# Squares of two chunks on row halves, V0 and V1 terms on quarters of the array, in a compressed-interaction kernel

## Chip, cores, metric

The kernel runs on one core of a Trainium2 chip. The metric is the device time of one execution in microseconds (us), the median of several runs. The profile adds TensorE's weight loads (PEld) to the engines PE (TensorE), DVE (VectorE), ACT (ScalarE), POOL (GpSimd) and SP (the queue of loads).

## The reference, cut to what matters

```python
def _cin_forward(x, Ws, bs, fc_w, fc_b, split_half=True):
    x0 = x; h = x; xs = []
    for i in range(3):                                   # cut
        z = jnp.einsum('bfe,bge->bfge', x0, h).reshape(Bn, f0 * fh, e)
        y = jnp.einsum('oc,bce->boe', Ws[i], z) + bs[i][None, :, None]
        if i != 2: x_i, h = y[:, :64, :], y[:, 64:, :]
        else:      x_i, h = y, y
        xs.append(x_i)
    return jnp.sum(jnp.concatenate(xs, axis=1), axis=2) @ fc_w.T + fc_b
```

x is 1024 x 64 x 16 in fp32, the hidden sizes are 64, the result is 1024 x 1. Everything after h1 is linear in the weights that follow, so the kernels fold W1, W2 and fc_w into one form M, and W0, W1 and fc_w into two 64 x 64 forms V0 and V1. What remains per element is h1 (64 rows), q = M(x, x) + V1 x (64 rows), and y = V0 x (64 rows): sum over (h1 + b) q + (y + c) x.

## The kernel before

The 32 batch rows of a chunk are laid out as 512 columns, there are 32 chunks. The 64 x 64 products x_f x_g are symmetric, so they are computed as 16 shifted products on 128 rows (`z`) and one square (the lower 64 rows of `zl`); each is multiplied by a 128 x 128 weight whose first 64 columns give h1 and whose last 64 give q.

```python
    def products(c, j):
        z = zp.tile([128, NI, N], F32, tag="z", name="z")
        nc.vector.tensor_tensor(z, xas[c], xbs[c][:, j, :]..., ALU.mult)
        for i in range(NI):
            t = j * NI + i
            nc.tensor.matmul(accs[c], w_all[:, t, :], z[:, i, :], start=(t == 0), stop=False)

    def squares(c):        # rows 0-63: x squared; rows 64-127: x itself, weights V1
        nc.scalar.activation(zls[c][0:64], xas[c][0:64, 0, :], AF.Square)
        nc.tensor.matmul(accs[c], w_all[:, NT, :], zls[c], start=False, stop=True)

    def combine(c):        # cut
        nc.scalar.copy(q, accs[c][64:128])
        nc.vector.scalar_tensor_tensor(uu[to, 0, :], accs[c][0:64], bh1, q, ALU.add, ALU.mult)
        if half == 0:
            return
        y = ps.tile([128, N], F32, tag="y", name=f"y_{c}", bufs=1)
        nc.tensor.matmul(y, bd, xxs[c // 2], start=True, stop=True)     # bd = diag(V0, V0)
        nc.vector.scalar_tensor_tensor(uu[:, 1, :], y, cx, xxs[c // 2], ALU.add, ALU.mult)
        nc.vector.tensor_reduce(acc[:, :, c // 2, :], uu..., AX.X, ALU.add)

    for c in range(NCH + 1):
        load_chunk(c + 1)                                   # cut: bounds
        products(c, 0); products(c, 1)
        combine(c - 1)
        products(c, 2); products(c, 3); squares(c)
```

The set-up makes the weights on the chip: `pv2` and `pm` matmuls (V2 form and M), M out to memory (`md`) and back in skewed form (`ms1`, `ms2`), summed into `w_all`; and V0 and V1 as one row:

```python
    for k in range(4):
        w01 = setup.tile([128, 1024], F32, tag="w01", name=f"w01_{k}")     # 2 buffers
        nc.sync.dma_start(out=w01, in_=wv01[:, k * 1024 : (k + 1) * 1024])
        for m in range(2):
            pv = ps.tile([2, 512], F32, tag="set", name=f"pv_{k}_{m}", bufs=4)
            nc.tensor.matmul(pv, fc01, w01[:, m * 512 : (m + 1) * 512], start=True, stop=True)
            nc.scalar.copy(vrow[:, col : col + 512], pv)
    # then transfers of vrow's two rows into w_all[64:128, NT, 64:128] (V1) and bd (V0, twice)
```

In the traces an engine's instructions don't always stand in the order of the source.

Of the kernel before, what the change touches and what calls it, by code (L numbers as in the profile page):

```python
# [23 lines left out]
F32 = mybir.dt.float32  # L27
AF = mybir.ActivationFunctionType
ALU = mybir.AluOpType
AX = mybir.AxisListType  # L30

F = 64
E = 16
B = 1024
CB = 32
N = CB * E
# [3 lines left out]
NT = NI * NJ  # L40
# [4 lines left out]
def cin_kernel(ctx, tc, x2, w0a, w0b, w1h, wv2, wv01, b0, b1, b2, fc_w, fc_b, out):  # L45
    nc = tc.nc
    const = ctx.enter_context(tc.tile_pool(name="const", bufs=1))
    setup = ctx.enter_context(tc.tile_pool(name="setup", bufs=2))
    xp = ctx.enter_context(tc.tile_pool(name="xp", bufs=3))
    zp = ctx.enter_context(tc.tile_pool(name="zp", bufs=3))  # L50
    sp = ctx.enter_context(tc.tile_pool(name="sp", bufs=2))
    ps = ctx.enter_context(tc.tile_pool(name="ps", bufs=2, space=bass.MemoryType.PSUM))
    dr = ctx.enter_context(tc.tile_pool(name="dr", bufs=1, space=bass.MemoryType.DRAM))

    def rows(c, first, dims):

        return bass.AP(
            tensor=x2.tensor,
            offset=(c * 2 * F + first) * N,
            ap=[[N, F]] + [[n * N, k] for n, k in dims] + [[1, N]],  # L60
        )
# [5 lines left out]
    nc.scalar.dma_start(out=fc2, in_=fc_w[0, 128:256].unsqueeze(1))  # L67
    nc.scalar.dma_start(out=fc01[0:64, 0:1], in_=fc_w[0, 0:64].unsqueeze(1))
    nc.scalar.dma_start(out=fc01[64:128, 1:2], in_=fc_w[0, 64:128].unsqueeze(1))
    bh1 = const.tile([F, 1], F32, tag="bh1", name="bh1")  # L70
    bh2 = const.tile([F, 1], F32, tag="bh2", name="bh2")
    bcol = const.tile([128, 2], F32, tag="bcol", name="bcol")
    fcol = const.tile([128, 2], F32, tag="fcol", name="fcol")
    fcb = const.tile([1, 1], F32, tag="fcb", name="fcb")
    b0c = b0.unsqueeze(1)
    b1c = b1.unsqueeze(1)
    nc.gpsimd.dma_start(out=bh1, in_=b0c[64:128])
    nc.gpsimd.dma_start(out=bh2, in_=b1c[64:128])
    nc.gpsimd.dma_start(out=bcol[0:64, 0:1], in_=b0c[0:64])
    nc.gpsimd.dma_start(out=bcol[64:128, 0:1], in_=b1c[0:64])  # L80
# [1 line left out]
    for j in range(2):  # L82
        nc.gpsimd.dma_start(
            out=fcol[:, j : j + 1], in_=fc_w[0, j * 128 : (j + 1) * 128].unsqueeze(1)
# [6 lines left out]
    nc.gpsimd.memset(ones[64:128, 1:2], 1.0)  # L91


    w_all = const.tile([128, NT + 1, 128], F32, tag="w_all", name="w_all")
    bd = const.tile([128, 128], F32, tag="bd", name="bd")
    nc.gpsimd.memset(w_all[64:128, NT, 0:64], 0.0)
    nc.gpsimd.memset(bd, 0.0)


    w2s = const.tile([128, 32, 128], F32, tag="w2s", name="w2s")  # L100
# [4 lines left out]
        nc.sync.dma_start(out=w2s[:, 8 * k : 8 * k + 8, :], in_=wv2[:, 8 * k : 8 * k + 8, :])  # L105
    nc.sync.dma_start(out=w1s, in_=w1h)

    xas, xbs, zls, xxs = {}, {}, {}, {}

    def load_chunk(c):  # L110
        xa = xp.tile([128, NI, N], F32, tag="xa", name=f"xa_{c}")
        xb = xp.tile([128, NJ, N], F32, tag="xb", name=f"xb_{c}")
        zl = xp.tile([128, N], F32, tag="zl", name=f"zl_{c}")
        for half in range(2):
            to = slice(half * F, (half + 1) * F)
            nc.sync.dma_start(out=xa[to], in_=rows(c, 0, [[1, NI]]))
            nc.sync.dma_start(out=xb[to], in_=rows(c, 16 * half + 4, [[4, NJ]]))
        nc.sync.dma_start(out=zl[F:128], in_=rows(c, 0, []))
        if c % 2 == 0:
            xxs[c // 2] = sp.tile([128, N], F32, tag="xx", name=f"xx_{c}")  # L120
        to = slice(c % 2 * F, (c % 2 + 1) * F)
        nc.sync.dma_start(out=xxs[c // 2][to], in_=rows(c, 0, []))
        xas[c], xbs[c], zls[c] = xa, xb, zl

    load_chunk(0)
    nc.sync.dma_start(out=w0t, in_=w0a)
# [1 line left out]


    v2t = const.tile([128, F], F32, tag="v2t", name="v2t")  # L130
    pv2 = ps.tile([128, 32], F32, tag="set", name="pv2", bufs=4)
    for k in range(32):
        nc.tensor.matmul(pv2[:, k : k + 1], w2s[:, k, :], fc2, start=True, stop=True)  # L133
    for half in range(2):
# [7 lines left out]
    for m in range(4):  # L142
        for half in range(2):
            to = slice(half * F, (half + 1) * F)
            pm = ps.tile([F, 512], F32, tag="set", name=f"pm_{m}_{half}", bufs=4)
            nc.tensor.matmul(  # L146
                pm, v2t[to], w1s[to, m * 512 : (m + 1) * 512], start=True, stop=True
            )
            f0 = half * 32 + m * 8
            m_to = m_sb[:, f0 : f0 + 8, :].rearrange("p f g -> p (f g)")  # L150
            if half:
                nc.vector.tensor_copy(m_to, pm)  # L152
            else:
                nc.scalar.copy(m_to, pm)
# [10 lines left out]
    def skewed(first, dims):  # L165
        return bass.AP(
            tensor=md.tensor, offset=md.offset + first, ap=[[row + F, F]] + dims
        )

    for half in range(2):  # L170
        to = slice(half * F, (half + 1) * F)
        b = 16 * half + 4
# [4 lines left out]
        for i in range(NI):  # L177
# [1 line left out]
                out=ms2[to].rearrange("p (j i) g -> p j i g", i=NI)[:, :, i, :],  # L179
                in_=skewed(i * row + b * F, [[4 * F, NJ], [1, F]]),  # L180
            )
    nc.scalar.dma_start(out=w_all[0:64, NT, 64:128], in_=skewed(0, [[1, F]]))

    nc.vector.memset(ms2[64:128, 3 * NI, :], 0.0)  # L184
    nc.vector.memset(w0u[64:128, 3 * NI, :], 0.0)
    nc.vector.tensor_tensor(w_all[:, 0:NT, 0:64], w0t[:, 0:NT, :], w0u, ALU.add)
    nc.vector.tensor_copy(w_all[0:64, NT, 0:64], w0t[0:64, NT, :])
    nc.vector.tensor_tensor(w_all[:, 0:NT, 64:128], ms1, ms2, ALU.add)  # L188


    vrow = const.tile([2, F * F], F32, tag="vrow", name="vrow")
    for k in range(4):
        w01 = setup.tile([128, 1024], F32, tag="w01", name=f"w01_{k}")
        nc.sync.dma_start(out=w01, in_=wv01[:, k * 1024 : (k + 1) * 1024])
        for m in range(2):
            pv = ps.tile([2, 512], F32, tag="set", name=f"pv_{k}_{m}", bufs=4)
            nc.tensor.matmul(pv, fc01, w01[:, m * 512 : (m + 1) * 512], start=True, stop=True)  # L197
            col = (2 * k + m) * 512
            nc.scalar.copy(vrow[:, col : col + 512], pv)  # L199
    nc.scalar.dma_start(  # L200
        out=w_all[64:128, NT, 64:128], in_=vrow[1:2, :].rearrange("o (f g) -> o f g", g=F)
    )
    for half in range(2):
        to = slice(half * F, (half + 1) * F)
        nc.scalar.dma_start(
            out=bd[to, to], in_=vrow[0:1, :].rearrange("o (f g) -> o f g", g=F)
        )


    cx = const.tile([128, 1], F32, tag="cx", name="cx")  # L210
    pcx = ps.tile([128, 1], F32, tag="set", name="pcx", bufs=4)
    for half in range(2):
        nc.tensor.matmul(
            pcx[half * F : (half + 1) * F], v2t[0:64], bh2, start=True, stop=True
        )
    nc.scalar.copy(cx, pcx)
    cst = const.tile([1, 1], F32, tag="cst", name="cst")
    pc = ps.tile([1, 1], F32, tag="set", name="pc", bufs=4)
    for j in range(2):
        nc.tensor.matmul(  # L220
            pc, fcol[:, j : j + 1], bcol[:, j : j + 1], start=(j == 0), stop=(j == 1)
# [2 lines left out]


    acc = const.tile([128, 2, NCH // 2, CB], F32, tag="acc", name="acc")
    accs, uus = {}, {}

    def products(c, j):
        z = zp.tile([128, NI, N], F32, tag="z", name="z")  # L230
        nc.vector.tensor_tensor(  # L231
            z, xas[c], xbs[c][:, j, :].unsqueeze(1).to_broadcast([128, NI, N]), ALU.mult
        )
        for i in range(NI):
            t = j * NI + i
            nc.tensor.matmul(accs[c], w_all[:, t, :], z[:, i, :], start=(t == 0), stop=False)  # L236

    def squares(c):
        nc.scalar.activation(zls[c][0:64], xas[c][0:64, 0, :], AF.Square)  # L239
        nc.tensor.matmul(accs[c], w_all[:, NT, :], zls[c], start=False, stop=True)  # L240

    def combine(c):
        half = c % 2
        to = slice(half * F, (half + 1) * F)
        if half == 0:
            uus[c // 2] = sp.tile([128, 2, N], F32, tag="uu", name=f"uu_{c}")
        uu = uus[c // 2]
        q = sp.tile([F, N], F32, tag="q", name=f"q_{c}")
        nc.scalar.copy(q, accs[c][64:128])  # L249
        nc.vector.scalar_tensor_tensor(uu[to, 0, :], accs[c][0:64], bh1, q, ALU.add, ALU.mult)  # L250
        if half == 0:
            return
        y = ps.tile([128, N], F32, tag="y", name=f"y_{c}", bufs=1)
        nc.tensor.matmul(y, bd, xxs[c // 2], start=True, stop=True)  # L254
        nc.vector.scalar_tensor_tensor(uu[:, 1, :], y, cx, xxs[c // 2], ALU.add, ALU.mult)  # L255
        nc.vector.tensor_reduce(  # L256
            acc[:, :, c // 2, :], uu.rearrange("p k (b e) -> p k b e", e=E), AX.X, ALU.add
        )

    for c in range(NCH + 1):  # L260
        if c + 1 < NCH:
            load_chunk(c + 1)
        if c < NCH:
            accs[c] = ps.tile([128, N], F32, tag="acc", name=f"acc_{c}")
            products(c, 0)
            products(c, 1)
        if c > 0:
            combine(c - 1)
        if c < NCH:
            products(c, 2)  # L270
            products(c, 3)
            squares(c)

    res = const.tile([1, B], F32, tag="res", name="res")
    half_pairs = NCH // 4
    for k in range(2):
        po = ps.tile([1, 2, half_pairs * CB], F32, tag="set", name=f"po_{k}", bufs=4)
        pairs = slice(k * half_pairs, (k + 1) * half_pairs)
        for half in range(2):
            for n in range(2):  # L280
                nc.tensor.matmul(  # L281
                    po[:, half, :],
                    ones[:, half : half + 1],
                    acc[:, n, pairs, :],
                    start=(half == 0 and n == 0),
                    stop=(half == 1 and n == 1),
                    skip_group_check=True,
                )
        nc.scalar.activation(  # L289
            res[:, k * 512 : (k + 1) * 512].rearrange("o (m h b) -> o h m b", h=2, b=CB),  # L290
            po.rearrange("o h (m b) -> o h m b", b=CB),
            AF.Identity,
            bias=cst,
        )
# [46 lines left out]
```

## Time and profile before

| | before |
|---|---|
| median of the runs | 554.62 us (552.36 to 554.69) |
| TensorE busy | 515.9 us of a span of 555.0 |
| VectorE, ScalarE busy | 352.0 and 44.9 us |
| first product matmul starts | 66.25 us |
| one pair of chunks in the loop | 30.04 us |

The lines that carry it are shown in the prediction. Read the table as two parts: a start of 66 us in which the weights are made, with TensorE waiting for more than half of it (31.3 us busy), and a loop in which TensorE never waits.

### The profile page before, as it was taken

To read this page: it belongs to the slowest core of one execution; us is meant where nothing else is said; L and a number is where in the kernel's file an instruction comes from. 1 tells how busy PE (TensorE), PEld (TensorE's weight loads), DVE (VectorE), ACT (ScalarE), POOL (GpSimd) and SP (SyncE) were. 2 spreads that over 40 slices of the span, in tenths; PEclk is the share of its full clock that TensorE was granted. 3 is DMA by queue.
4 is the path that set the end of the run, shared out by engine and by line. 5 is a ranking of instruction groups with operands and counts; after the bars stand their busy time and mean duration, and the time that the engine had idled before them with its cause. 6 is when DMAs were issued, how large, how long until landed. Compare 5 with 4: busy or idle time off the path is not lost.

```text
span 555.0 us, 3402 instructions
## 1 busy us (share of the span) xinstructions
PE 515.9 (93%) x1240; PEld 231.9 (42%) x1240; DVE 352.0 (63%) x205; ACT 44.9 (8%) x81; POOL 5.3 (1%) x18
## 2 busy tenths in 40 slices
PE   5803799999999999999999999999999999999997
PEld 5600144444444444444444444444444444444442
DVE  0250076768677677768676867767776867686751
ACT  0100300000000000000000000000000000000001
POOL 3000000000000000000000000000000000000000
PEclk9967699999999999999999999999999999999999
DMA  8999998787777777877778777777787877874000
GB/s 254 185 283 210 205 208 170 144 163 146 156 153 159 150 152 162 180 161 161 160 147 165 146 154 154 154 150 154 161 180 161 165 155 151 162 152 77 0 1 0
DMA packets 33114, 85.33 MB, mean 154 GB/s; under 512 B 6405, under 2 KB 6949, under 8 KB 28710
## 3 DMA queue, kind: packets, MB, share of 16 engines
q1 hardware_dynamic: 29234, 81.84, 71.1%
q10 hardware_dynamic: 3608, 3.28, 2.8%
q8 instruction: 10, 0.16, 0.2%
q14 instruction: 6, 0.05, 0.0%
q0 software_dynamic: 256, 0.00, 0.0%
HBM read 82.89 MB, written 2.17 MB: 153 GB/s over the span
## 4 chain that ended last, share of the span: by engine, by line
PE 92%; DMA 6%; DVE 0%; ACT 0%; issue 0%; ACTq 0%; SPq 0%
PE acc L236 79%; PE acc L240 5%; DMA w<-in_wv 3%; PE pv L133 2%; PE y L254 2%; PE pv L197 2%; DMA ms<-md 1%; DMA fc<-in_fc_w 1%; DMA md<-m_sb 1%; PE pm L146 1%; PE po L281 0%; DVE acc L256 0%; DVE uu L255 0%; ACT res L289 0%; ACT q L249 0%
## 5 line engine op out<-in xcount | busy, mean ns | idle before, releaser
L236 PE MATMUL acc<-z,w_all 128*128 128x512 f32 x1024 | 447.2, 592 | 0.0
L231 DVE TENSOR_TENSOR z<-xa,xb 128x2048 f32<-128x2048 f32 x128 | 293.3, 2292 | 135.9 <-PE acc L236 134.6
L236 PEld LDWEIGHTS acc<-z,w_all 128*128 128x128 f32 x1024 | 194.5, 190 | 244.5 <-issue 244.4
L249 ACT COPY q<-acc 64x512 f32<-64x512 f32 x32 | 18.6, 582 | 443.8 <-PE acc L240 443.8
L197 PE MATMUL pv<-w,fc 128*2 128x512 f32 x16 | 11.5, 887 | 27.9 <-DMA w<-in_wv 14.9
L240 PE MATMUL acc<-zl,w_all 128*128 128x512 f32 x64 | 32.7, 592 | 0.0
L250 DVE SCALAR_TENSOR_TENSOR uu<-acc,bh,q 64x512 f32<-64x512 f32 x32 | 23.7, 740 | 10.0 <-ACT q L249 9.5
L239 ACT ACTIVATE zl<-xa 64x512 f32<-64x512 f32 x32 | 20.1, 628 | 3.6 <-DMA xa<-in_x 3.6
L133 PE MATMUL pv<-fc,w2s 128*128 128x1 f32 x64 | 13.8, 352 | 6.6 <-DMA fc<-in_fc_w 6.6
L256 DVE TENSOR_REDUCE acc<-uu 128x64 f32<-128x1024 f32 x16 | 19.5, 1220 | 0.5
L240 PEld LDWEIGHTS acc<-zl,w_all 128*128 128x128 f32 x64 | 12.2, 190 | 15.3 <-issue 15.3
L197 PEld LDWEIGHTS pv<-w,fc 128*2 128x2 f32 x16 | 1.6, 108 | 37.6 <-issue 21.5
L133 PEld LDWEIGHTS pv<-fc,w2s 128*128 128x128 f32 x64 | 13.7, 332 | 6.6 <-DMA fc<-in_fc_w 6.6
L254 PE MATMUL y<-xx,bd 128*128 128x512 f32 x32 | 16.3, 592 | 0.0
L136 DVE COPY v2t<-pv 64x32 f32<-64x32 f32 x2 | 0.4, 184 | 20.4 <-PE pv L133 20.4
L255 DVE SCALAR_TENSOR_TENSOR uu<-y,cx,xx 128x512 f32<-128x512 f32 x16 | 11.9, 745 | 0.0
L188 DVE TENSOR_TENSOR w_all<-ms,ms 128x1024 f32<-128x1024 f32 x1 | 1.2, 1224 | 13.2 <-DMA ms<-md 13.2
L254 PEld LDWEIGHTS y<-xx,bd 128*128 128x128 f32 x32 | 6.1, 190 | 7.7 <-issue 7.7
L199 ACT COPY vrow<-pv 2x512 f32<-2x512 f32 x8 | 4.2, 570 | 33.3 <-DMA ms<-md 32.2
L184 DVE MEMSET ms<- 64x64 f32 x1 | 0.1, 112 | 9.7 <-DMA ms<-md 9.7
L146 PE MATMUL pm<-w1s,v2t 64*64 64x512 f32 x16 | 5.6, 809 | 0.5 <-DVE v2t L137 0.5
L152 DVE COPY m_sb<-pm 64x512 f32<-64x512 f32 x4 | 2.7, 683 | 3.2 <-PE pm L146 3.2
(33 smaller groups left out, 21.0 us busy)
## 6 DMA issues: line engine op xcount, KB each, us to landing
xa<-in_x SPq DMA_DIRECT2D x64, 512.0 KB, 5.8
xb<-in_x SPq DMA_DIRECT2D x64, 512.0 KB, 7.1
zl<-in_x SPq DMA_DIRECT2D x32, 128.0 KB, 4.2
xx<-in_x SPq DMA_DIRECT2D x32, 128.0 KB, 4.1
w2s<-in_wv SPq DMA_DIRECT2D x4, 512.0 KB, 7.8
w<-in_wv SPq DMA_DIRECT2D x4, 512.0 KB, 11.9
w1s<-in_w1h SPq DMA_DIRECT2D x1, 1024.0 KB, 13.4
md<-m_sb ACTq DMA_DIRECT2D x2, 512.0 KB, 7.1
```

Source lines behind the costliest of these rows:

```text
L133: nc.tensor.matmul(pv2[:, k : k + 1], w2s[:, k, :], fc2, start=True, stop=True)
L146: nc.tensor.matmul(pm, v2t[to], w1s[to, m * 512 : (m + 1) * 512], start=True, stop=True)
L197: nc.tensor.matmul(pv, fc01, w01[:, m * 512 : (m + 1) * 512], start=True, stop=True)
L231: nc.vector.tensor_tensor(z, xas[c], xbs[c][:, j, :].unsqueeze(1).to_broadcast([128, NI, N]), ALU.mult)
L236: nc.tensor.matmul(accs[c], w_all[:, t, :], z[:, i, :], start=(t == 0), stop=False)
L239: nc.scalar.activation(zls[c][0:64], xas[c][0:64, 0, :], AF.Square)
L240: nc.tensor.matmul(accs[c], w_all[:, NT, :], zls[c], start=False, stop=True)
L249: nc.scalar.copy(q, accs[c][64:128])
L250: nc.vector.scalar_tensor_tensor(uu[to, 0, :], accs[c][0:64], bh1, q, ALU.add, ALU.mult)
L254: nc.tensor.matmul(y, bd, xxs[c // 2], start=True, stop=True)
L255: nc.vector.scalar_tensor_tensor(uu[:, 1, :], y, cx, xxs[c // 2], ALU.add, ALU.mult)
L256: nc.vector.tensor_reduce(acc[:, :, c // 2, :], uu.rearrange("p k (b e) -> p k b e", e=E), AX.X, ALU.add)
```

## The change

The intent: TensorE spends 35 full matmuls a pair of chunks, 32 on products, 2 on squares (whose lower 64 rows carry V1) and 1 on y. Squares alone need 64 rows, V0 and V1 need 64 rows and 64 columns each. So the change squares both chunks of a pair at once and runs the two squares matmuls on the two row halves of the array side by side, and the four V terms (V0 and V1 of two chunks) on its four quarters: 34 units instead of 35. For the four V terms to fall on four different quarters the odd chunk must have its h1 and q halves swapped, which needs a third block of weight columns.

```diff
-    w_all = const.tile([128, NT + 1, 128], F32, tag="w_all", name="w_all")
-    bd = const.tile([128, 128], F32, tag="bd", name="bd")
+    w_all = const.tile([128, NT, 192], F32, tag="w_all", name="w_all")   # h1 | q | h1
+    w_sq = const.tile([128, 128], F32, tag="w_sq", name="w_sq")
+    w_x = const.tile([128, 128], F32, tag="w_x", name="w_x")
 ...
+    nc.scalar.copy(w_all[:, :, 128:192], w_all[:, :, 0:64])
 ...     # set-up PSUM tiles: bufs=4 becomes bufs=3; accumulators: 2 become 4
-            pv = ps.tile([2, 512], F32, tag="set", name=f"pv_{k}_{m}", bufs=4)
+            pv = ps.tile([2, 512], F32, tag="set", name=f"pv_{k}_{m}", bufs=3)
 ...
+    def begin(k):
+        xx = xxs[k]
+        sq = sp.tile([128, N], F32, tag="sq", name=f"sq_{k}")
+        nc.scalar.activation(sq, xx, AF.Square)
+        ys[k] = ps.tile([128, N], F32, tag="y", name=f"y_{k}", bufs=1)
+        for half in range(2):
+            to = slice(half * F, (half + 1) * F)
+            acc_c = ps.tile([128, N], F32, tag="acc", name=f"acc_{2 * k + half}", bufs=4)
+            accs[2 * k + half] = acc_c
+            nc.tensor.matmul(acc_c, w_sq[to], sq[to], start=True, stop=False, ...)
+        for half in range(2):
+            to = slice(half * F, (half + 1) * F)
+            other = slice((1 - half) * F, (2 - half) * F)
+            nc.tensor.matmul(ys[k][to], w_x[to, to], xx[to], start=True, stop=True)
+            nc.tensor.matmul(accs[2 * k + half][other], w_x[to, other], xx[to],
+                             start=False, stop=False, ...)
 ...
     for c in range(NCH + 1):
 ...
+            if c % 2 == 0:
+                begin(c // 2)
             products(c, 0)
             products(c, 1)
         if c > 0:
             combine(c - 1)
         if c < NCH:
             products(c, 2)
             products(c, 3)
-            squares(c)
```

The y matmul goes out of `combine`, whose VectorE product with y moves to the even chunk. The loads of `zl` (128 KB a chunk) go. I call the squares and quarters of `begin` "the block" from here on.

More of the change, by code (lines that the diff above doesn't have):

```diff
@@ L69, in cin_kernel @@
     nc.scalar.dma_start(out=fc01[64:128, 1:2], in_=fc_w[0, 64:128].unsqueeze(1))
-    bh1 = const.tile([F, 1], F32, tag="bh1", name="bh1")
+    bh1 = const.tile([128, 1], F32, tag="bh1", name="bh1")
     bh2 = const.tile([F, 1], F32, tag="bh2", name="bh2")
@@ L76, in cin_kernel @@
     b1c = b1.unsqueeze(1)
-    nc.gpsimd.dma_start(out=bh1, in_=b0c[64:128])
+    for half in range(2):
+        nc.gpsimd.dma_start(out=bh1[half * F : (half + 1) * F], in_=b0c[64:128])
     nc.gpsimd.dma_start(out=bh2, in_=b1c[64:128])
@@ L91, in cin_kernel @@
     nc.gpsimd.memset(ones[64:128, 1:2], 1.0)
-    w_all = const.tile([128, NT + 1, 128], F32, tag="w_all", name="w_all")
-    bd = const.tile([128, 128], F32, tag="bd", name="bd")
-    nc.gpsimd.memset(w_all[64:128, NT, 0:64], 0.0)
-    nc.gpsimd.memset(bd, 0.0)
+    w_all = const.tile([128, NT, 192], F32, tag="w_all", name="w_all")
+    w_sq = const.tile([128, 128], F32, tag="w_sq", name="w_sq")
+    w_x = const.tile([128, 128], F32, tag="w_x", name="w_x")
     w2s = const.tile([128, 32, 128], F32, tag="w2s", name="w2s")
@@ L106, in cin_kernel @@
     nc.sync.dma_start(out=w1s, in_=w1h)
-    xas, xbs, zls, xxs = {}, {}, {}, {}
+    xas, xbs, sqs, xxs = {}, {}, {}, {}
     def load_chunk(c):
@@ L112, in load_chunk @@
         xb = xp.tile([128, NJ, N], F32, tag="xb", name=f"xb_{c}")
-        zl = xp.tile([128, N], F32, tag="zl", name=f"zl_{c}")
         for half in range(2):
@@ L117, in load_chunk @@
             nc.sync.dma_start(out=xb[to], in_=rows(c, 16 * half + 4, [[4, NJ]]))
-        nc.sync.dma_start(out=zl[F:128], in_=rows(c, 0, []))
         if c % 2 == 0:
@@ L122, in load_chunk @@
         nc.sync.dma_start(out=xxs[c // 2][to], in_=rows(c, 0, []))
-        xas[c], xbs[c], zls[c] = xa, xb, zl
+        xas[c], xbs[c] = xa, xb
     load_chunk(0)
@@ L130, in cin_kernel @@
     v2t = const.tile([128, F], F32, tag="v2t", name="v2t")
-    pv2 = ps.tile([128, 32], F32, tag="set", name="pv2", bufs=4)
+    pv2 = ps.tile([128, 32], F32, tag="set", name="pv2", bufs=3)
     for k in range(32):
@@ L144, in cin_kernel @@
             to = slice(half * F, (half + 1) * F)
-            pm = ps.tile([F, 512], F32, tag="set", name=f"pm_{m}_{half}", bufs=4)
+            pm = ps.tile([F, 512], F32, tag="set", name=f"pm_{m}_{half}", bufs=3)
             nc.tensor.matmul(
@@ L181, in cin_kernel @@
             )
-    nc.scalar.dma_start(out=w_all[0:64, NT, 64:128], in_=skewed(0, [[1, F]]))
+    for half in range(2):
+        to = slice(half * F, (half + 1) * F)
+        nc.scalar.dma_start(out=w_sq[to, (1 - half) * F : (2 - half) * F], in_=skewed(0, [[1, F]]))
     nc.vector.memset(ms2[64:128, 3 * NI, :], 0.0)
     nc.vector.memset(w0u[64:128, 3 * NI, :], 0.0)
-    nc.vector.tensor_tensor(w_all[:, 0:NT, 0:64], w0t[:, 0:NT, :], w0u, ALU.add)
-    nc.vector.tensor_copy(w_all[0:64, NT, 0:64], w0t[0:64, NT, :])
-    nc.vector.tensor_tensor(w_all[:, 0:NT, 64:128], ms1, ms2, ALU.add)
+    nc.vector.tensor_tensor(w_all[:, :, 0:64], w0t[:, 0:NT, :], w0u, ALU.add)
+    nc.scalar.copy(w_all[:, :, 128:192], w_all[:, :, 0:64])
+    for half in range(2):
+        to = slice(half * F, (half + 1) * F)
+        nc.vector.tensor_copy(w_sq[to, to], w0t[to, NT, :])
+    nc.vector.tensor_tensor(w_all[:, :, 64:128], ms1, ms2, ALU.add)
     vrow = const.tile([2, F * F], F32, tag="vrow", name="vrow")
@@ L199, in cin_kernel @@
             nc.scalar.copy(vrow[:, col : col + 512], pv)
-    nc.scalar.dma_start(
-        out=w_all[64:128, NT, 64:128], in_=vrow[1:2, :].rearrange("o (f g) -> o f g", g=F)
-    )
     for half in range(2):
         to = slice(half * F, (half + 1) * F)
-        nc.scalar.dma_start(
-            out=bd[to, to], in_=vrow[0:1, :].rearrange("o (f g) -> o f g", g=F)
-        )
+        for v in range(2):
+            at = (half + v) % 2 * F
+            nc.scalar.dma_start(
+                out=w_x[to, at : at + F],
+                in_=vrow[v : v + 1, :].rearrange("o (f g) -> o f g", g=F),
+            )
     cx = const.tile([128, 1], F32, tag="cx", name="cx")
-    pcx = ps.tile([128, 1], F32, tag="set", name="pcx", bufs=4)
+    pcx = ps.tile([128, 1], F32, tag="set", name="pcx", bufs=3)
     for half in range(2):
@@ L217, in cin_kernel @@
     cst = const.tile([1, 1], F32, tag="cst", name="cst")
-    pc = ps.tile([1, 1], F32, tag="set", name="pc", bufs=4)
+    pc = ps.tile([1, 1], F32, tag="set", name="pc", bufs=3)
     for j in range(2):
@@ L226, in cin_kernel @@
     acc = const.tile([128, 2, NCH // 2, CB], F32, tag="acc", name="acc")
-    accs, uus = {}, {}
+    accs, uus, qs, ys = {}, {}, {}, {}
+    def begin(k):
[3 more added lines that the diff above has]
+        ys[k] = ps.tile([128, N], F32, tag="y", name=f"y_{k}", bufs=1)
+        for half in range(2):
+            to = slice(half * F, (half + 1) * F)
+            acc_c = ps.tile([128, N], F32, tag="acc", name=f"acc_{2 * k + half}", bufs=4)
+            accs[2 * k + half] = acc_c
+            nc.tensor.matmul(
+                acc_c, w_sq[to], sq[to], start=True, stop=False, skip_group_check=True
+            )
+        for half in range(2):
+            to = slice(half * F, (half + 1) * F)
+            other = slice((1 - half) * F, (2 - half) * F)
+            nc.tensor.matmul(ys[k][to], w_x[to, to], xx[to], start=True, stop=True)
+            nc.tensor.matmul(
+                accs[2 * k + half][other], w_x[to, other], xx[to],
+                start=False, stop=False, skip_group_check=True,
+            )
     def products(c, j):
@@ L233, in products @@
         )
+        first = c % 2 * F
         for i in range(NI):
             t = j * NI + i
-            nc.tensor.matmul(accs[c], w_all[:, t, :], z[:, i, :], start=(t == 0), stop=False)
-    def squares(c):
-        nc.scalar.activation(zls[c][0:64], xas[c][0:64, 0, :], AF.Square)
-        nc.tensor.matmul(accs[c], w_all[:, NT, :], zls[c], start=False, stop=True)
+            nc.tensor.matmul(
+                accs[c], w_all[:, t, first : first + 128], z[:, i, :],
+                start=False, stop=(t == NT - 1), skip_group_check=True,
+            )
     def combine(c):
-        half = c % 2
+        k, half = divmod(c, 2)
         to = slice(half * F, (half + 1) * F)
+        other = slice((1 - half) * F, (2 - half) * F)
         if half == 0:
-            uus[c // 2] = sp.tile([128, 2, N], F32, tag="uu", name=f"uu_{c}")
-        uu = uus[c // 2]
-        q = sp.tile([F, N], F32, tag="q", name=f"q_{c}")
-        nc.scalar.copy(q, accs[c][64:128])
-        nc.vector.scalar_tensor_tensor(uu[to, 0, :], accs[c][0:64], bh1, q, ALU.add, ALU.mult)
-        if half == 0:
-            return
-        y = ps.tile([128, N], F32, tag="y", name=f"y_{c}", bufs=1)
-        nc.tensor.matmul(y, bd, xxs[c // 2], start=True, stop=True)
-        nc.vector.scalar_tensor_tensor(uu[:, 1, :], y, cx, xxs[c // 2], ALU.add, ALU.mult)
-        nc.vector.tensor_reduce(
-            acc[:, :, c // 2, :], uu.rearrange("p k (b e) -> p k b e", e=E), AX.X, ALU.add
-        )
+            uus[k] = sp.tile([128, 2, N], F32, tag="uu", name=f"uu_{k}")
+            qs[k] = sp.tile([128, N], F32, tag="q", name=f"q_{k}")
+            nc.vector.scalar_tensor_tensor(
+                uus[k][:, 1, :], ys[k], cx, xxs[k], ALU.add, ALU.mult
+            )
+        uu, q = uus[k], qs[k]
+        nc.scalar.copy(q[to], accs[c][other])
+        nc.vector.scalar_tensor_tensor(
+            uu[to, 0, :], accs[c][to], bh1[to], q[to], ALU.add, ALU.mult
+        )
+        if half:
+            nc.vector.tensor_reduce(
+                acc[:, :, k, :], uu.rearrange("p k (b e) -> p k b e", e=E), AX.X, ALU.add
+            )
     for c in range(NCH + 1):
@@ L263, in cin_kernel @@
         if c < NCH:
-            accs[c] = ps.tile([128, N], F32, tag="acc", name=f"acc_{c}")
+            if c % 2 == 0:
+                begin(c // 2)
             products(c, 0)
@@ L276, in cin_kernel @@
     for k in range(2):
-        po = ps.tile([1, 2, half_pairs * CB], F32, tag="set", name=f"po_{k}", bufs=4)
+        po = ps.tile([1, 2, half_pairs * CB], F32, tag="set", name=f"po_{k}", bufs=3)
         pairs = slice(k * half_pairs, (k + 1) * half_pairs)
```

## The prediction

> **What bounds the kernel now.** I read the page from the top: engines, slices, chain, groups; then the critical chain in order of time, the windows of the steady loop, and the timeline at the two ends. First the page's busy line, the slices and the chain.
>
> ```profile
> PE 515.9 (93%) x1240; PEld 231.9 (42%) x1240; DVE 352.0 (63%) x205; ACT 44.9 (8%) x81; POOL 5.3 (1%) x18
> ...
> PE   5803799999999999999999999999999999999997
> ...
> PEclk9967699999999999999999999999999999999999
> ...
> PE 92%; DMA 6%; DVE 0%; ACT 0%; issue 0%; ACTq 0%; SPq 0%
> ```
>
> TensorE is busy 93% of the span and is 92% of the chain that ended last. What it does not fill lies in the first five of the 40 slices (13.9 us each), where the granted clock also falls. The windows view (columns: stretch, length, busy time per engine, then granted clock, DMA share, GB/s) has the steady loop:
>
> ```profile
> 0.00:66.25 66.25, 31.28 (x104) 17.97 (x105) 12.87 (x16) 7.70 (x13) 5.25 (x18) 0.79 0.97 227
> ...
> 132.61:222.73 90.12, 90.12 (x211) 39.90 (x211) 64.85 (x36) 6.68 (x12) 0.00 (x0) 1.00 0.78 158
> ```
>
> From 132.61 to 222.73 us, the starts of two y matmuls three pairs of chunks apart, TensorE has no gap: 90.12/3 = 30.04 us a pair. A pair has 32 product matmuls, 2 squares and 1 y, 35 in all; 30.04/35 = 0.858 us for one full fp32 matmul of 512 columns, which the trace holds as two instructions 0.429 us apart. VectorE is busy 65 of those 90 us. So the loop is TensorE's, and any time on it counts one for one: 16 x 30.04 = 481 us of the 554.6.
>
> The start is another matter: 66.25 us pass before the first product. The chain in order of time:
>
> ```profile
> 59.61 6.33 PE pv L197 x8
> 65.94 0.21 PE pcx L213 x4
> 66.15 0.17 PE pc L220 x4
> 66.32 13.93 PE acc L236 x32
> 80.25 0.86 PE acc L240 x2
> ```
>
> and ScalarE in the same stretch, where the row made of V0 and V1 (vrow) is finished and sent into the weights:
>
> ```profile
> 67.38 0.63 ACT L239 ACTIVATE zl<-xa 64x512 f32<-64x512 f32 x1 [3.58 <-DMA xa<-in_x]
> 67.91 1.03 ACT L199 COPY vrow<-pv 2x512 f32<-2x512 f32 x2
> ...
> 68.98 0.53 ACTq L200 DMA_DIRECT2D w_all<-vrow  x1
> 69.60 1.20 ACTq L205 DMA_DIRECT2D bd<-vrow  x2
> ```
>
> The reader should see that the products start at 66.3 us, before vrow is even complete (67.91 + 1.03 = 68.94). Its transfers are needed only by the squares at 80.25 us, and y comes later still.
>
> **What the Trainium skill says.** (1) "TensorE: Matmul & The Clock Gate", Part 3: matmuls on different row and column groups run concurrently in the array, with measured gains below the ideal, and their starts stay in program order. (2) "TensorEngine Tiling (Array Packing)", Key Properties: "Changing tiling mode (not just tile) drains the TensorE"; the same page, Gotcha 1, says that different row tiles cannot access the same PSUM bank simultaneously. (3) "TensorE: Matmul & The Clock Gate", Part 1: an idle TensorE falls back to half clock after some 3.4 us and needs as long a busy window to come back. The trace agrees with (3): 59.6 to 65.1 us has a granted clock of 0.50 after a long idle time. On (1) it has one witness, the set-up matmuls pm: 64 rows by 64 columns, two of them on row half 0, then two on row half 1. [...]
>
> ```profile
> 21.76 0.23 PEld L146 LDWEIGHTS pm<-w1s,v2t 64*64 64x64 f32 x1 [0.20 <-issue]
> 22.18 0.23 PEld L146 LDWEIGHTS pm<-w1s,v2t 64*64 64x64 f32 x1 [0.20 <-issue]
> 22.61 0.23 PEld L146 LDWEIGHTS pm<-w1s,v2t 64*64 64x64 f32 x1 [0.20 <-issue]
> ```
> ```profile
> 42.21 0.13 PEld L197 LDWEIGHTS pv<-w,fc 128*2 128x2 f32 x1 [0.72 <-issue]
> 43.07 0.13 PEld L197 LDWEIGHTS pv<-w,fc 128*2 128x2 f32 x1 [0.72 <-issue]
> 43.92 0.13 PEld L197 LDWEIGHTS pv<-w,fc 128*2 128x2 f32 x1 [0.72 <-issue]
> ```
>
> Both stretches run slow (single matmuls of about 1.06 us, against 0.59 later). Half-row instructions come 0.43 us apart, full-row ones 0.86. So row halves give the factor of two: 0.2145 us an instruction at full clock. No run of pm uses the second column half, so whether quarters give four is not shown. On (2): between the last pv (its second start is at about 65.35, stream 0.43, so done at 65.78) and pcx at 65.87 there is 0.1 us of nothing, and the first product after pc takes 0.53 us to its successor instead of 0.43. I read a mode change as 0.1 us of drain and 0.1 us of an exposed weight load, 0.2 us together.
>
> **The change part by part.** Per pair it takes away 2 squares and 1 y: 3 x 0.858 = 2.575 us of TensorE. It puts in a block X, once a pair:
> - two squares matmuls on row halves, 4 instructions x 0.2145 = 0.86 us;
> - four quarter matmuls (V0 and V1 of two chunks), 8 instructions. At the half-row rate 8 x 0.2145 = 1.72 us; if column halves overlap too, 0.86. Midway, 1.29;
> - three mode changes (full to halves, to quarters, to full) x 0.2 = 0.6 us.
> X = 0.86 + 1.29 + 0.6 = 2.75 us, so a pair gets 0.18 us longer; 16 pairs: +2.8 us. With everything ideal X is 1.72 and the change saves 16 x 0.86 = 13.7 us (2.5%); that is its intent, 34 units in place of 35.
>
> The end: the last y's 0.86 us lay beside the chain of q and uu before, so it is not saved; but the y product on VectorE (0.75 us and its gap, 0.78) leaves the chain. Sum about 0.
>
> The start: squares and V terms now open each accumulator, so the first product waits for the V weights. They are four transfers rather than three, about 0.6 us of issue each from 68.98, the last issued at 70.8; landing took 6.4 to 7.1 us for the three of before: 77.5 us. The earlier first product was at 66.25, a gap of 11.3. The squares part of the first block, about 1.1 us with its drain, fits into the waiting: 10.2 us net. Against it, the Square that kept ScalarE waiting 3.58 us before the last vrow copies may fall elsewhere (-1.5). For it: set-up has 3 PSUM buffers, not 4, so only three pv run before ScalarE copies the first at 59 us, and the last w01 load, waiting for the fourth pv, goes out after 61 us where it went at 46.6; a copy of 128x1024 is added on ScalarE, some 1.2 us. I set +2.3 for these: 11 us. TensorE idles about 10 us there, so its clock falls; 3.4 to 6.8 us at half clock lose 1.7 to 3.4: +2. Start: +13 us.
>
> Elsewhere: a transfer of 128 KB a chunk goes (32 x 128 KB of 85 MB, 5%), but no TensorE time waits for it in the loop. ScalarE does 16 squares of 128 rows rather than 32 of 64, at 8% busy. The copy q and both products on VectorE keep their sizes; one moves to the even chunk, where it can run while waiting. The pair's second half of xx must land before the block; its load follows one chunk behind VectorE, which itself runs up to three z tiles (10 us) ahead of TensorE, so about 20 us are in hand against some 12 of transfers.
>
> Sum: 554.6 + 2.8 + 13 = 570.4; I say 570.
>
> **The rivals.**
> 1. Quarters run four at once and a mode change is hidden: X = 1.72, -13.7 us. For it: the skill's tiling gains, and the author's careful swap that gives each of the four terms its own quarter. Against it: each fp32 matmul is two instructions on the same quarter one after the other, starts stay in order, and the two V0 quarters write one PSUM bank from two row halves. With a start delay of 10 the time is 551; with none 541.
> 2. Quarters do not overlap by columns and each mode change also waits for the staggered second instruction: X about 3.4, +13 us; with the start 581.
> 3. The weights' order at the start is arranged differently (vrow earlier, its loads less crowded), so the delay is 3 to 5 us instead of 13: 561.
> 4. The loop becomes bound by a late xx or a late Square: nothing in the waits speaks for it now; it would add a gap before every block.
>
> **Range and chances.** The start can cost 4 to 20 us, the loop -10 to +14. I take 570 with 553 to 584 for 8 in 10. Faster by over 2% (below 543.5) needs ideal quarters and almost no delay: 0.07. Slower by over 2% (above 565.7) needs +11: the start alone nearly does it, 0.60. Within 2%: 0.33.
>
> **What would show it.** In the changed profile: the first product's start near 79 us (the start step) and the wait in front named as vrow's transfer; the distance between blocks of neighbouring pairs, 30.2 us against 30.04 (X); starts in a quarter block 0.21 or 0.11 us apart; gaps of 0.2 us at mode changes; a low clock just after the first products. A pair of 29.2 us and a first product before 70 us would make the prediction wrong on the fast side; a pair over 31 us on the slow side.

## The result, and the profile after

The changed kernel takes 571.02 us (570.31 to 571.18, 4 runs) against 554.62: ratio 1.0303, 95% interval 1.0276 to 1.0331. It is slower, and the number is about a microsecond from the 570 foretold. Its two terms were further off: the trace shows that the loop got faster, and the start lost more than the whole difference.

The page of the changed kernel, the lines that answer to those of before:

```profile
PE 522.5 (92%) x1336; PEld 221.9 (39%) x1336; DVE 352.4 (62%) x206; ACT 39.1 (7%) x66; POOL 5.5 (1%) x17
...
PE   5821579999999999999999999999999999999997
...
PEclk9975668999999999999999999999999999999999
...
PE 90%; DMA 8%; ACT 1%; DVE 0%; ACTq 0%; issue 0%
```

The slices are of 14.2 us now. TensorE is full from the seventh slice on, where it was from the sixth; the low clock reaches into the seventh, where it used to end in the fifth; and transfers take 8% of the chain where they took 6%. Behind that the picture is as full as before. The windows view of the changed kernel separates the two parts (columns as in the prediction):

```profile
79.18:90.18 11.00, 11.00 (x16) 3.29 (x17) 0.75 (x1) 1.06 (x2) 0.00 (x0) 0.53 0.13 27
114.62:144.36 29.74, 29.74 (x78) 12.58 (x78) 21.63 (x12) 1.79 (x3) 0.00 (x0) 1.00 0.72 150
```

**The loop.** From the second pair's block to the third's is 29.74 us, without a gap, against 30.04 before. 32 products are 32 x 0.858 = 27.47 us, so the block costs 29.74 - 27.47 = 2.27 us and replaces 2.575. The timeline of one block (start, busy us, engine, line, operation, count):

```profile
144.29 1.13 PE L245 MATMUL acc<-sq,w_sq 64*128 64x512 f32 x4
...
145.35 0.64 PE L251 MATMUL y<-xx,w_x 64*64 64x512 f32 x1
...
145.36 0.64 PE L252 MATMUL acc<-xx,w_x 64*64 64x512 f32 x1
...
145.37 0.64 PE L251 MATMUL y<-xx,w_x 64*64 64x512 f32 x1
...
145.37 0.64 PE L252 MATMUL acc<-xx,w_x 64*64 64x512 f32 x1
...
145.83 0.59 PE L251 MATMUL y<-xx,w_x 64*64 64x512 f32 x1
...
146.37 0.70 PE L265 MATMUL acc<-z,w_all 128*128 128x512 f32 x1
```

The first instructions of all four quarter matmuls start within 0.02 us of each other, the second ones 0.48 us later, and the products go on 1.02 us after the first. So four quarters stream at once: two instruction lengths, 0.86 us, for eight instructions. The squares take 1.06 us in the same way on two row halves. Four instruction lengths are 1.716 us; what is left of 2.27 is 0.56 us, for three mode changes: 0.186 us each.

**The start.** The chain of waits of the changed kernel in order of time:

```profile
61.50 1.88 PE pv L203 x2
...
63.40 9.18 DMA w<-in_wv
...
72.71 3.59 PE pv L203 x4
...
76.92 2.21 DMA w_x<-vrow
...
79.18 1.49 PE y L251 x2
80.66 1.11 PE acc L252 x2
81.77 2.00 PE acc L265 x2
83.77 1.04 PE y L251
```

The fourth pv matmul waits for ScalarE's copy and runs at 61.5 us. Only then can the last w01 load go out (63.40) into the buffer that this matmul frees. It lands 9.18 us later; the last pv matmuls, ScalarE's copies and the w_x transfers follow, and the first quarters start at 79.18 us. Until then no product runs: the squares have opened the first accumulator at 66.4 us, but its V1 term stands in front of its products in the program. The first product starts at 81.70 us in place of 66.25. Then comes a second loss, which the first window above shows: the granted clock is 0.53 from 79.18 to 90.18. The clock records of the trace have half clock from 79.70 to 89.94 us, so 10.24 us do the work of 5.12. In this stretch the trace also has two product instructions (2.0 us) between the first and the second chunk's quarters, so the quarters of the first block take from 79.18 to 85.6, 6.4 us, where a later block takes 2.27 with its squares.

Together: before, the third chunk starts at 95.5 us; after, the second pair's block starts at 114.6. That is 19.1 us lost. The fifteen pairs left give back 15 x 0.30 = 4.5 us and the end 1.1 us (0.78 of it the y product, which no longer follows the last product on VectorE): 19.1 - 4.5 - 1.1 = 13.5, the difference of the two profiled spans, 568.5 and 555.0. The medians differ by 16.4: the profiled run of before, at 556.77 us, was 2.15 above its median, and that of the change, at 570.31, was 0.71 below. What made those 2.9 us isn't known.

### The profile page after: what moved, and what is told of

It reads as the page before. It is cut to its first block, busy times and chain, and to the rows that moved or that the text cites. A ratio compares the mean times of both kernels' runs of the same rounds, so it can differ in the third digit from the quotient of the medians.

```text
span 568.5 us, 3474 instructions
## 1 busy us (share of the span) xinstructions
PE 522.5 (92%) x1336; PEld 221.9 (39%) x1336; DVE 352.4 (62%) x206; ACT 39.1 (7%) x66; POOL 5.5 (1%) x17
## 4 chain that ended last, share of the span: by engine, by line
PE 90%; DMA 8%; ACT 1%; DVE 0%; ACTq 0%; issue 0%
PE acc L265 78%; DMA xb<-in_x 3%; PE y L251 3%; PE acc L245 3%; PE pv L134 2%; DMA md<-m_sb 2%; DMA w<-in_wv 2%; PE pm L147 1%; PE pv L203 1%; DMA fc<-in_fc_w 1%; DMA w_x<-vrow 0%; PE po L311 0%; PE acc L252 0%; DVE acc L286 0%; ACTq L179 0%
## 5 line engine op out<-in xcount | busy, mean ns | idle before, releaser
L203 PE MATMUL pv<-w,fc 128*2 128x512 f32 x16 | 14.0, 1027 | 32.9 <-DMA w<-in_wv 19.1
L251 PE MATMUL y<-xx,w_x 64*64 64x512 f32 x64 | 19.7, 636 | 2.5 <-DMA w_x<-vrow 2.5
L252 PE MATMUL acc<-xx,w_x 64*64 64x512 f32 x64 | 20.2, 644 | 0.0
L245 PE MATMUL acc<-sq,w_sq 64*128 64x512 f32 x64 | 19.1, 641 | 0.0
L239 ACT ACTIVATE sq<-xx 128x512 f32<-128x512 f32 x16 | 10.1, 630 | 99.3 <-DMA xx<-in_x 96.9
L245 PEld LDWEIGHTS acc<-sq,w_sq 64*128 64x128 f32 x64 | 5.1, 184 | 13.6 <-issue 12.2
L251 PEld LDWEIGHTS y<-xx,w_x 64*64 64x64 f32 x64 | 3.5, 133 | 15.5 <-issue 12.9
L147 PE MATMUL pm<-w1s,v2t 64*64 64x512 f32 x16 | 6.9, 874 | 0.5 <-DVE v2t L138 0.5
```

Of the source, the lines that this page charges most:

```text
L147: nc.tensor.matmul(pm, v2t[to], w1s[to, m * 512 : (m + 1) * 512], start=True, stop=True)
L245: nc.tensor.matmul(acc_c, w_sq[to], sq[to], start=True, stop=False, skip_group_check=True)
L251: nc.tensor.matmul(ys[k][to], w_x[to, to], xx[to], start=True, stop=True)
L252: nc.tensor.matmul(accs[2 * k + half][other], w_x[to, other], xx[to], start=False, stop=False, skip_group_check=True,)
```

## The experiments

The theory at this point (A): the block is cheaper than what it replaces, and all of the loss is the start, where the products wait for weights that were not urgent before. The main rival: the block, or its place, costs time of its own in the loop. Smaller questions are whether the four quarters really overlap, what a mode change costs, and which wait makes the V weights late.

| kernel | median us | ratio to before | first product, us | pair, us |
|---|---|---|---|---|
| before | 554.62 | 1 | 66.25 | 30.04 |
| the change | 571.02 | 1.0303 | 81.70 | 29.74 |
| block between the two chunks | 556.76 | 1.0060 | 64.97 | 29.74 |
| four set-up PSUM buffers | 563.93 | 1.0196 | 75.25 | 29.74 |
| four w01 buffers | 564.62 | 1.0195 | 76.05 | 29.74 |
| without V1 (wrong result) | 559.19 | 1.0109 | 69.10 | 29.73 |
| late block, four set-up buffers | 552.78 | 0.9993 | 67.77 | 29.74 |
| the same, squares in quarters | 549.65 | 0.9932 | 67.54 | 29.54 |
| the change, squares in quarters | 564.80 | 1.0218 | 77.99 | 29.54 |
| early block, early V weights | 555.62 | 1.0046 | 71.63 | 29.74 |
| late block in quarters, early V weights | 550.94 | 0.9955 | 65.55 | 29.54 |
| early block, all weights early | 552.27 | 0.9970 | 68.11 | 29.74 |
| the same, squares in quarters | 546.88 | 0.9872 | 66.05 | 29.54 |

The last two columns are read from the start times in the traces. All results but the one marked are correct. The kernel before was run again beside each group, with medians between 552.7 and 554.6 us, so the ratios are the safer comparison.

### 1. The block between the two chunks of a pair

```diff
             if c % 2 == 0:
-                begin(c // 2)
+                accs[c] = ps.tile([128, N], F32, tag="acc", name=f"acc_{c}", bufs=4)
+            else:
+                begin(c // 2)       # adds to the even chunk's sum, opens the odd chunk's
```

> The changed kernel with its block of squares and V terms moved from before a pair's first chunk to between its two chunks, so that the first products need no V weights. Theory A (the loop of the change is shorter, 29.74 us a pair against 30.04, and the whole loss is the start, some 19 us to the second pair): the first product starts near 66 us as in the kernel before, the pair stays at 29.74, the total is about 549 us, 1% under the kernel before. Rival (the block costs more than it saves wherever a real wait for it shows, or in the middle of a pair it delays the sums of the even chunk): pairs of 30.2 us or more, total 555 or above.

Measured: 556.76 us, ratio 1.006 (1.0041 to 1.0080). The first product starts at 64.97 us and the pair is 29.74 us, both as theory A has it, but the total is 8 us over what it foretold and lies in the rival's range. The pair speaks against the rival. The timeline of this run says where most of the 8 us are:

```profile
64.97 3.70 PE L266 MATMUL acc<-z,w_all 128*128 128x512 f32 x8
...
72.15 1.88 PE L203 MATMUL pv<-w,fc 128*2 128x512 f32 x4 [3.48 <-DMA w<-in_wv]
...
74.34 10.57 PE L266 MATMUL acc<-z,w_all 128*128 128x512 f32 x24
```

The last pv matmuls now stand behind the first eight product instructions. They wait 3.48 us for the late w01 load, and the other products come after them, at 74.34 us. The first pair takes 35.8 us by this, 6.0 more than the later ones. So the start has two causes, not one: the place of the block, and the late load.

### 2 and 3. The late load: PSUM buffers or SBUF buffers

Four set-up buffers in PSUM again, with three accumulators in place of four:

```diff
-            pv = ps.tile([2, 512], F32, tag="set", name=f"pv_{k}_{m}", bufs=3)
+            pv = ps.tile([2, 512], F32, tag="set", name=f"pv_{k}_{m}", bufs=4)   # and all others of "set"
-            acc_c = ps.tile(..., name=f"acc_{2 * k + half}", bufs=4)
+            acc_c = ps.tile(..., name=f"acc_{2 * k + half}", bufs=3)
```

> The changed kernel with four set-up PSUM buffers again, as before (accumulators three in place of four). Theory A1 (the third buffer's loss made the fourth pv wait for ScalarE, hence the last w01 load go out at 63.4 us and not at about 47, hence V weights late): the last w01 load is out before 50 us, the first product of the whole run starts at 72 to 74 us in place of about 82, total 562 to 565 us. Rival (ScalarE's own order, its added copy and Square, sets the V weights): under 2 us gained, total 569 or more.

Or, alone, four buffers for the loads:

```diff
-    setup = ctx.enter_context(tc.tile_pool(name="setup", bufs=2))
+    setup = ctx.enter_context(tc.tile_pool(name="setup", bufs=4))
```

> The changed kernel with four SBUF buffers for the w01 loads in place of two, PSUM as it is (three). Theory A1: the last load no longer waits for a pv matmul, so it lands early; the pv matmuls still queue behind ScalarE's copies from 61 us, V weights at about 71 to 73 us, total 562 to 566 us. Rival (the PSUM buffers themselves, not the load, hold the pv matmuls): as the changed kernel, 569 or more.

Measured: 563.93 and 564.62 us, both inside the totals that theory A1 expected. The last load now goes out at 46.4 and at 36.6 us, so either buffer is enough to free it, and it is worth about 7 us. The first product comes at 75.25 and 76.05 us; in the first of the two runs 72 to 74 was expected, and one part of the miss is that the first w_x transfer, at 68.3 us, now takes 4.6 us to land, where the change had 2.2. The pair is 29.74 us in both, so three accumulators do as well as four there.

### 4. Without the V1 quarters

```diff
-            nc.tensor.matmul(
-                accs[2 * k + half][other], w_x[to, other], xx[to],
-                start=False, stop=False, skip_group_check=True,
-            )
```

> The changed kernel without its two V1 quarter matmuls (the result is wrong on purpose; two quarters of the array stay empty). Theory Q (four quarter matmuls stream side by side): the loop keeps 29.74 us a pair and the total stays within 1.5 us of the changed kernel's 571. Rival (row halves overlap, column halves do not, as the prediction half assumed): a pair is 0.43 to 0.86 us shorter, total 557 to 564.

The result is wrong, on purpose. The chain of this run in order of time:

```profile
105.12 27.66 PE acc L261 x64
...
134.84 5.35 PE acc L261 x12
```

A pair is 29.72 us here (29.73 over ten pairs): two of the four quarter matmuls left out save 0.01 to 0.02 us. So the two V1 quarters run entirely beside the two V0 quarters, as the starts in the timeline said. The total, 559.19 us, missed its expectation of 571 by 12 us, and that miss is useful: without V1 no V weight stands in front of the accumulators, the products start at 69.1 us, and the low clock after the wait goes with it. So having the V1 term in front of the products cost some 12 us, the low clock included. That is not all of the wait for the V weights: the late w01 load still holds TensorE for 1.53 us (to 72.61) here, with the last pv matmuls behind the first four product instructions, and the first pair takes 36.0 us.

### 5, 6, 7. Both causes together; the price of a mode change

The late block with four set-up buffers:

> The block between the two chunks and four set-up PSUM buffers together (the changed kernel otherwise). Theory A (two separate causes at the start: the place of the block and the late w01 load): no gap after the first eight products, where the run with the late block alone still had one of 3.4 us and the last pv matmuls behind it; first product near 66 us, pairs of 29.74 us, total 549 to 551 us, 0.6 to 1% under the kernel before. Rival (the start has another cause, or the gains overlap): 554 or more.

Measured: 552.78 us, ratio 0.9993 (0.9971 to 1.0015), 1.8 us over the expected range. The gap is gone, the pair is 29.74 us, and the first product is at 67.77 us. It is still 1.5 us later than before: ScalarE's added copy of w_all (1.04 us) stands in front of its vrow copies, and those in front of the pv matmuls. Of the four combinations of block and buffers (571.0, 563.9, 556.8 and 552.8 us) the buffers gain 7.1 alone, the place 14.3, both 18.2: the waits overlap in part.

Then the squares in quarters as well, so that the whole block has one mode:

```diff
-            nc.tensor.matmul(
-                accs[2 * k + half], w_sq[to], sq[to],
-                start=(half == 1), stop=False, skip_group_check=True,
-            )
+            for at in (to, slice((1 - half) * F, (2 - half) * F)):
+                nc.tensor.matmul(
+                    accs[2 * k + half][at], w_sq[to, at], sq[to],
+                    start=(half == 1), stop=False, skip_group_check=True,
+                )
```

> As the run before it, and the squares are split by columns too, so that the whole block runs in quarters: two mode changes a pair instead of three. Theory M (a mode change costs about 0.19 us, whatever the two modes): pairs of 29.55 us, total 3 us under the run before it, 546 to 548. Rival (the cost is that of coming from and going to the full array; between halves and quarters there is none): pairs of 29.74, same total.

The chain of this run:

```profile
83.41 27.66 PE acc L267 x64
111.08 1.02 PE acc L246 x8
...
112.95 27.67 PE acc L267 x64
```

A pair is 112.95 - 83.41 = 29.54 us, 0.20 less than 29.74, and the total 549.65 us (ratio 0.9932), 3.1 less, as theory M has it; it is 1.65 over the range of 546 to 548, as the run it builds on was over its own. The change between halves and quarters costs what the other changes cost. The same edit in the changed kernel as it was, with its block in front:

> The changed kernel with only its squares split by columns (quarters all through the block), block and buffers as in the change. Theory M: pairs of 29.55 us in place of 29.74, total about 568, the start unchanged (the first products still wait for the V weights). Rival: 571, pairs unchanged.

The pair is 29.54 us again. The total, 564.80, is 3 us better than expected: in this run the same late w01 load, nothing of which was edited, landed in 5.34 us instead of 9.18 (at 70.6 in place of 72.6 us), the last pv matmuls ran in 1.89 us at full clock instead of 3.59, and the first product came 3.7 us earlier. Why the load was quicker isn't shown.

### 8 and 9. The V weights made early

The block in its first place, but without its wait. The vrow copies and the w_all copy go to VectorE, which otherwise waits from 49.6 to 63.9 us (late block with four set-up buffers), and the w_x transfers to GpSimd's queue; set-up buffers are four. The sum into w_all's q columns and the memset in front of it move behind the vrow copies on VectorE (not shown in the cut). These edits were not made one by one.

```diff
-            nc.scalar.copy(vrow[:, col : col + 512], pv)
+            nc.vector.tensor_copy(vrow[:, col : col + 512], pv)
...
-            nc.scalar.dma_start(out=w_x[to, at : at + F], ...)
+            nc.gpsimd.dma_start(out=w_x[to, at : at + F], ...)
```

> The change's block where the change has it, before the pair's first chunk, but the V weights made early: the vrow copies and the copy of w_all on the idle VectorE in place of ScalarE (which stands behind its queue of transfers until 59 us), the V weights' transfers on GpSimd's queue, four set-up PSUM buffers. Theory A (an early block costs nothing if its weights are there): the block starts near 66 us, held by the second half of xx or by the w_all sum, not by V weights; pairs 29.74; total 550 to 553, some 20 us under the change. Rival (a block in front of the first product costs its wait whatever the weights): 560 or more.

Measured: 555.62 us, 8 under the same kernel with late V weights, but 3 over the expected range. The chain names the next wait:

```profile
58.54 9.13 DMA w_sq<-md
...
67.72 2.07 PE acc L246 x2
...
71.70 28.40 PE acc L266 x64
```

The weights of the squares, issued last in ScalarE's queue, land at 67.7 us and hold the block in their turn. The late block in quarters with the same early V weights:

> The best version so far (late block, quarters throughout, four set-up PSUM buffers) with the same early V weights. The first product should come near 66 us in place of 67.6, the pairs stay at 29.54: 546.5 to 549, one to two us under the best so far and about 1% under the kernel before. If the queue of ScalarE did not hold the start, no change: 549.5 or more.

Measured: 550.94 us, over the expected 546.5 to 549 and no better than the 549.65 without. The first product did move from 67.54 to 65.55 us, but the ninth product instruction starts at 71.39 us here and at 71.07 there. The windows of those eight instructions, first of this run, then of the run without early V weights:

```profile
65.54:71.39 5.85, 5.84 (x8) 2.55 (x9) 0.61 (x1) 0.00 (x0) 0.00 (x0) 0.60 0.91 179
```
```profile
67.53:71.07 3.54, 3.54 (x11) 1.63 (x9) 0.00 (x0) 0.51 (x3) 0.00 (x0) 1.00 1.02 195
```

The clock is 0.60 in the first and 1.00 in the second. The reading that fits: with late V weights the pv matmuls run from 61.4 us up to the products, and the clock is back at 65.96; with early ones TensorE waits between the y quarters (to 63.8) and the products, and the clock is back at 70.23 only. No run tests this alone. A first product's time says little without the clock that follows it.

### 10 and 11. All weights early

The w_sq transfers go to GpSimd's queue as well:

```diff
-        nc.scalar.dma_start(out=w_sq[to, (1 - half) * F : (2 - half) * F], in_=skewed(0, [[1, F]]))
+        nc.gpsimd.dma_start(out=w_sq[to, (1 - half) * F : (2 - half) * F], in_=skewed(0, [[1, F]]))
```

> The early block with early V weights, and now also the squares' weights (w_sq) on GpSimd's queue, since the run before it showed the block held until 67.7 us by the second w_sq transfer, issued last in ScalarE's queue. Theory A (an early block costs nothing once every weight of it is there): the block runs before the w_all sum ends near 65.4 us, the first product follows at 65.5 to 66.5 us in place of 71.6, in a low clock for its first few us; total 549 to 552. Rival (an early block costs by its place): 555 or more.

Measured: 552.27 us, 0.3 over the range. The first product is at 68.11 us, later than foretold, since the block itself runs from 62.3 us at half clock. With the squares in quarters too:

> The same with the squares in quarters: pairs of 29.54 us, 3 us less than the run before it, 546 to 549; it shows whether an early block with early weights or the late block (549.65) is the better.

Measured: 546.88 us, ratio 0.9872 (0.9841 to 0.9904), inside the range and 5.4 under the run before it: 3.2 are 16 pairs of 0.20 less, 2.1 an earlier first product. It is 1.3% under the kernel before and 24 us under the change, with the block exactly where the change put it. Here the first product starts at 66.05 us and the clock is back at 65.36. So no cost of the block's place shows once its weights are there (the late block was not run with all weights early); what cost was the weights that it waited for, and the clock that stayed low after the wait. These two were not changed apart.

## Why the prediction was right, and where only its sum was

- *TensorE bounds the loop, the rest is the start.* Right, and still so after the change.
- *The change takes away 2.575 us a pair.* Right: 32 products are still 27.47 of the 29.74 us.
- *Squares on row halves 0.86 us.* Right: 1.06 us from start to start, one mode change of 0.19 included. The set-up matmuls pm have the rate at full clock too: four starts are 0.214 to 0.216 us apart from 24.26 us on.
- *A mode change costs 0.2 us.* Right: 0.186 us from the block, 0.20 from taking one away (29.74 to 29.54). The set-up matmuls gave 0.1 us before and 0.1 after a change; in the block of 144.29 us the starts have 0.09 to 0.11 extra before and 0.05 to 0.11 after each of the three.
- *Quarters 1.29 us, midway between 0.86 and 1.72.* Wrong size: 0.86. The pm matmuls could show two row halves only, and I split the difference for the columns: this term is the one that turned the loop's gain into a loss. Four quarters overlap fully; without V1 the pair stays at 29.73. So X is 2.27, not 2.75 us, and the loop gains 16 x 0.30 = 4.8 us where I had it lose 2.8.
- *The first product waits for the V weights, near 79 us.* The mechanism was right and named by the chain: 81.70 us, w_x<-vrow in front. Its parts were not. The transfer landed in 2.2 us where I took 6.7, at a DMA share of 0.14 (76.92 to 79.13 us) where before it was 1.03 (68.98 to 77.00); the late w01 load, one item in my +2.3, held 9.2 us on the chain, and removing it is worth 7 us.
- *The clock falls, +2 us.* Mis-sized: 10.24 us at half clock, 5.1 us lost. I had counted at most 6.8 us of it.
- *The end about 0 beyond the loop's account.* Right: from the end of the last product to the end of the span 9.70 us before, 7.91 after; 0.86 of the 1.79 is the square that the loop's account has, 0.78 the y product.

On the account of the prediction the start cost 13.5 + 4.8 = 18.3 us between the two traces (21.2 by the medians), where it said 13. So the loop's error (7.6 us, on the slow side) and the start's (5 us by the traces and 8 by the medians, on the fast side) nearly cancelled. The range and the chances were honest for that; the closeness of 570 to 571 was luck. Rival 1, that quarters run four at once, was right about the quarters and wrong about the mode changes, which are not hidden.

Left open: why the clock stayed low for 10.24 us after 79.70 us, with TensorE busy all the while, and came back after some 3.5 us of work in the last experiment. The traces show more than that. In all thirteen, up to the loop, the clock keeps one value for 3.41 us or a multiple of it; 10.24 us are three such windows. TensorE is busy for the whole of the first two (79.70 to 83.11 and 83.11 to 86.53 us), but each holds 1.9 us or more in which only one chunk's quarters run, on one row half by the program. The third, 86.53 to 89.94, has full products alone, and the clock comes back at its end. The run of experiment 10 looks alike: 62.13 to 65.54 us has one quarter alone for 1.9 us and the clock stays low; 65.54 to 68.96 has both row halves at work, and it comes back. So busy time alone doesn't explain it, and the share of the rows at work would fit; no run changes that alone.

## What to carry to other kernels

When a term is moved to the front of an accumulation, everything it needs becomes urgent: list the weights, and the load, copy and queue behind each, before counting what the array saves. Here small fp32 matmuls that filled the array together were worth their full share (four quarters in 0.86 us), less some 0.19 us per change of shape, so group them in as few shapes as possible. In the start of a kernel look at first work and clock together: TensorE, after its wait, ran 10.24 us at half clock here.

## What the Trainium skill lacked or had wrong

- "TensorEngine Tiling (Array Packing)" says that a mode change drains TensorE (Key Properties), but not how long that takes: here 0.186 to 0.20 us for each change, between full array, row halves and quarters alike, the exposed first weight load included. It also says that different row tiles cannot access the same PSUM bank simultaneously (Gotcha 1); the two y quarters, on different row halves and different column halves, write one bank, start 0.02 us apart or less (145.35 and 145.37 us), and the result is correct. The point is against the wording of this page, for whole banks; not all of the skill puts it so widely.
- "TensorE: Matmul & The Clock Gate", Part 3, gives gains for 32-row and 32-column tiles, all below the ideal. For fp32 quarters of 64 x 64 with 512 columns, which it doesn't give, the overlap is complete: eight instructions in two instruction lengths, 0.86 us, beside the price of the mode changes.
- The same page, Part 1, gives some 3.4 us of sustained work for the clock to come back. The last experiment agrees (work from 61.83, full clock at 65.36 us); the changed kernel does not: work from 79.18, full clock at 89.94 us, with two whole windows of 3.41 us of busy TensorE before the one that brought it back. That work on part of the array may count for less is not on the page, and not shown here either.
